# Queries and keys of the second attention: transposed in 32x32 blocks by VectorE and moved through DRAM, in place of TensorE transposes

## The chip, the cores and the metric

The kernel runs on one core of one Trainium2 chip. The core has TensorE (PE, matrix products, with its weight loads listed as PEld), VectorE (DVE), ScalarE (ACT), GpSimd (POOL) and SyncE (SP, which here only issues DMAs). Sixteen DMA engines move data between DRAM and the on-chip memory SBUF, and within SBUF. Matrix products are written to PSUM, which DMA does not touch here. The metric is the device time in microseconds (us) of one execution. All arithmetic is in 32-bit floats, in which a matrix product is issued as two passes.

## The reference

The input x has 8 sequences (b) of 128 tokens with 512 features. A first attention with small heads follows a per-sequence weight matrix, and its output is added to x. The second attention, on which the change bears, has 32 query heads and 8 key/value heads (groups) of 128 features, with a cache of 512 keys a sequence before the 128 own ones:

```python
q = jnp.einsum('bsd,ed->bse', x, Wq).reshape(bsz, seqlen, HQ, D)
k = jnp.einsum('bsd,ed->bse', x, Wk).reshape(bsz, seqlen, HK, D)
v = jnp.einsum('bsd,ed->bse', x, Wv).reshape(bsz, seqlen, HK, D)
q = _rmsnorm(q, q_norm_w)
k = _rmsnorm(k, k_norm_w)
q = _rope(q, pos)
k = _rope(k, pos)
kc = k_cache[block_table].reshape(bsz, L, HK, D)
vc = v_cache[block_table].reshape(bsz, L, HK, D)
k_all = jnp.concatenate([kc, k], axis=1)
v_all = jnp.concatenate([vc, v], axis=1)
scores = jnp.einsum('bqhd,bkhd->bhqk', q, k_all) * SCALE
scores = jnp.where(valid[:, None, None, :], scores, -1e+30)
probs = jax.nn.softmax(scores, axis=-1)
o = jnp.einsum('bhqk,bkhd->bqhd', probs, v_all)
return jnp.einsum('bse,de->bsd', o.reshape(bsz, seqlen, HQ * D), Wo)
```

Its output goes through a feed-forward layer (a dense matrix plus low-rank LoRA terms that depend on the sequence), whose result is added again.

## The kernel before

**Units.** The second attention is cut into 64 units (L141). A unit u is one group g of 4 query heads and one key/value head, for one sequence b. Units come in pairs: 2n and 2n+1 are two neighbouring groups of the same sequence, whose cached keys and values lie side by side and are gathered together by GpSimd (L149 to L166, four indirect DMAs for the keys and four for the values of a pair). The sequences run inside, the pairs of groups outside; so the weights of two groups are in use for 16 units, and the next two are loaded in time (L110 to L116).

**Order.** Every engine executes its instructions in the order in which the program writes them; there is no planner. The loop at L1052 is a software pipeline written by hand. In iteration u it writes the scores of unit u (L866), into which the projection of the queries of unit u+1 is woven (`between`, L1057, over `q_matmul`, L172), then the projection of keys and values of u+1 (L217), then the product of the probabilities of unit u-1 with the values (L956), and the output projection of u-1 (L976). In the last group the feed-forward of a finished sequence follows (L1007 to L1048) in every odd iteration from 51 on.

**A unit's steps.** The projected queries lie in PSUM as 128 tokens x 4 heads x 128 features. `q_turn` (L185) rotates them with tables of cosines and sines, already multiplied by the norm's weight, that stay in SBUF for all sequences (`ca`, `sa`, L110): three multiplications on VectorE, one addition on GpSimd, and the squares for the norm on ScalarE. `kv_turn` (L221) does the same for the keys. `norms` (L238) makes the factors from the squares, with a power on GpSimd between two steps of VectorE; the keys are scaled, the queries' factor is kept for the scores. The score product needs features on the partitions. So `queries` (L250) transposes the four heads on TensorE into PSUM (L254) and ScalarE copies them to SBUF (L256); `own_keys` (L268) does the same for the 128 own keys (L271, L273).

**Cached keys.** From unit 4 on they are transposed without TensorE: `turn_keys` (L834) has VectorE transpose them in 32x32 blocks, in odd iterations, behind `norms`; `move_keys` (L850) then moves the blocks to their partitions with 16 DMAs between SBUF tiles for a pair, 8 in each of two units, issued by SP after the third head's reduction (L923).

**Scores.** For each head r two products, with the queries as the stationary operand: 512 cached keys (L889) and 128 own keys (L896). VectorE adds the mask, scales and takes the row's minimum in one instruction (L902); ScalarE takes exponentials with their sum (L912) and divides (L880). PSUM has two buffers for scores, so the third head's product waits for the first head's reduction. VectorE then transposes the probabilities in blocks (L883), and 16 DMAs (L936) move the blocks to their partitions; the products with the values (L963), one iteration later, need all of them. In the last unit TensorE transposes the probabilities instead (L941).

**Behind the values.** VectorE copies the result out of PSUM (L971), TensorE multiplies it with the output weights (L982), and the sum over groups is kept in SBUF: copied by ScalarE for group 0 (L987), added by VectorE for the others (L989).

**Buffers.** The large intermediate tiles share a ring of 12 buffers (`tile_a`, L90). The first attention uses the same ring for the gathered weight matrices (`gather_w`, L292) and for the LoRA weights (`merge_loads`, L420).

## Time and profile before

| | us |
|---|---|
| median of 3 runs (1421.93 to 1422.63) | 1422.53 |
| the profiled execution | 1423.96 |
| its span, first to last instruction | 1421.1 |
| first score product of unit 0 | 220.6 |
| period of a unit in the middle | 17.8 |
| PE busy | 1391.5 |
| DVE busy | 931.8 |
| ACT busy | 655.9 |
| POOL busy | 568.2 |

The mean granted clock of TensorE is 0.997 of full speed. In a line of a group, the numbers after the bar are the busy time in us, the mean duration of one instruction in ns, and, after the next bar, the idle time of the engine just before them with what ended most of it. In a line of the timeline the columns are start in us, duration in us, engine, line, operation, the tiles (written <- read), the shape, and how many instructions were merged; in square brackets the engine's idle time before it and what ended it. A matmul's end is modelled and overlaps with the next one, so the distance from start to start says what it costs. "128*128" is the part of the array in use.

### The profile page before, as it was taken

The page shows a single profiled execution, that of the slowest core. Times are in us where ns is not written, and L with a number is a line of the kernel's source. Part 1 is how long each engine was busy: PE and PEld are TensorE (multiplying, and loading weights), DVE is VectorE, ACT ScalarE, POOL GpSimd, SP SyncE. Part 2 cuts the span into 40 slices and gives each one's busy share as a digit, 9 for nine tenths or more (in the row PEclk, how much of TensorE's full clock was granted, in tenths as well). Part 3 has the DMA queues.
Part 4 walks back from the last instruction along what each step waited for, and adds up shares of the span by engine and source line. Part 5 has one row for each costly group of instructions (what it writes and reads, how often), then busy time and mean ns, then how long its engine had stood idle before and what let it go on. Part 6 is the DMA issues. An engine that isn't in the chain of part 4 may idle for free.

```text
span 1421.1 us, 20290 instructions
## 1 busy us (share of the span) xinstructions
PE 1391.5 (98%) x6244; PEld 898.5 (63%) x6244; DVE 931.8 (66%) x2266; ACT 655.9 (46%) x1520; POOL 568.2 (40%) x553
## 2 busy tenths in 40 slices
PE   6999989999999999999999999999999999999998
PEld 6877755566666666666666666666666665666555
DVE  5777846566666666666666666666666665666651
ACT  3555535444444444444444444444444444344431
POOL 5774342433333333333333333333333433343220
PEclk9999999999999999999999999999999999999999
DMA  6255013444444565444445654444456544444440
GB/s 198 75 164 183 31 37 104 129 117 118 119 115 119 161 193 151 119 119 119 119 119 159 196 148 119 118 119 119 121 160 192 152 117 136 131 111 112 115 111 30
DMA packets 156202, 180.26 MB, mean 127 GB/s; under 512 B 92416, under 2 KB 97792, under 8 KB 156096
## 3 DMA queue, kind: packets, MB, share of 16 engines
q1 hardware_dynamic: 140544, 134.39, 34.0%
q0 software_dynamic: 15552, 44.58, 10.8%
q8 instruction: 50, 0.82, 0.2%
q14 instruction: 56, 0.46, 0.1%
HBM read 75.83 MB, written 4.72 MB: 57 GB/s over the span
## 4 chain that ended last, share of the span: by engine, by line
PE 93%; DVE 2%; issue 2%; DMA 1%; ACT 1%; POOL 1%; SPq 1%; another core or an unknown queue 0%; DVEq 0%; POOLq 0%; ACTq 0%
PE op L963 19%; PE qp L177 15%; PE sc L889 15%; PE yp L982 15%; PE kvp L217 7%; PE sc L896 4%; PE fp L1044 2%; PE hp L514 2%; PE qTp L254 2%; PE pT1p L638 2%; PE qp L530 2%; PE att L673 2%; PE o L657 1%; PE sc L595 1%; PE kvp L545 1%
## 5 line engine op out<-in xcount | busy, mean ns | idle before, releaser
L902 DVE CUSTOM_DVE_ANT_0 pr<-sc,mask,nq 128x640 f32<-128x640 f32 x256 | 226.0, 884 | 144.2 <-PE sc L896 90.9
L912 ACT ACTIVATE pr<-pr,nm 128x640 f32<-128x640 f32 x256 | 211.8, 827 | 189.3 <-DVE nm L902 102.1
L889 PE MATMUL sc<-kT,qT 128*128 128x512 f32 x512 | 262.0, 593 | 0.0
L177 PE MATMUL qp<-wq,x1T 128*128 128x512 f32 x512 | 251.2, 593 | 0.0
L963 PE MATMUL op<-pT,vg 128*128 128x256 f32 x1024 | 242.0, 379 | 1.6 <-DMA pT<-fl 1.6
L203 POOL TENSOR_TENSOR qa<-qa,qb 128x512 f32<-128x512 f32 x64 | 81.8, 1278 | 375.2 <-DVE sums L879 375.2
L982 PE MATMUL yp<-wo,oT 128*128 128x512 f32 x504 | 229.2, 598 | 2.0 <-DVE oT L971 2.0
L963 PEld LDWEIGHTS op<-pT,vg 128*128 128x128 f32 x1024 | 193.9, 190 | 27.8 <-DVE sums L879 1.8
L880 ACT ACTIVATE pr<-pr,sums 128x640 f32<-128x640 f32 x256 | 208.4, 814 | 0.0
L883 DVE STREAM_TRANSPOSE fl<-pr 128x640 f32<-128x640 f32 x252 | 189.2, 808 | 0.0
L896 PEld LDWEIGHTS sc<-kTo,qT 128*128 128x128 f32 x512 | 96.4, 190 | 124.4 <-issue 119.2
L982 PEld LDWEIGHTS yp<-wo,oT 128*128 128x128 f32 x504 | 91.4, 191 | 95.1 <-issue 91.5
L160 POOL DMA_INDIRECT kg<-in_k_cache_dram,idx_kv x128 | 131.6, 1029 | 35.3 <-issue 34.8
L160 POOL DMA_INDIRECT vg<-in_v_cache_dram,idx_kv x128 | 128.6, 1005 | 37.8 <-issue 33.6
L889 PEld LDWEIGHTS sc<-kT,qT 128*128 128x128 f32 x512 | 87.7, 191 | 80.2 <-issue 77.8
L256 ACT COPY qT<-qTp 128x512 f32<-128x512 f32 x64 | 37.5, 586 | 205.3 <-PE qTp L254 204.7
L217 PEld LDWEIGHTS kvp<-wkv,x1T 128*128 128x128 f32 x512 | 97.3, 190 | 40.5 <-issue 30.1
L217 PE MATMUL kvp<-wkv,x1T 128*128 128x256 f32 x512 | 121.0, 379 | 0.0
L244 POOL TENSOR_TENSOR rs<-ss,minus_half 128x5 f32<-128x5 f32 x64 | 76.5, 1196 | 83.1 <-DVE ss L242 82.2
L177 PEld LDWEIGHTS qp<-wq,x1T 128*128 128x128 f32 x512 | 82.8, 191 | 31.5 <-issue 31.5
L896 PE MATMUL sc<-kTo,qT 128*128 128x128 f32 x512 | 99.2, 275 | 0.0
L273 ACT COPY kTo<-kTp 128x128 f32<-128x128 f32 x64 | 17.1, 267 | 166.4 <-issue 115.2
(155 smaller groups left out, 1701.1 us busy)
## 6 DMA issues: line engine op xcount, KB each, us to landing
pT<-fl SPq DMA_DIRECT2D x1008, 80.0 KB
kT<-flk SPq DMA_DIRECT2D x480, 32.0 KB
wq<-in_wq_dram SPq DMA_DIRECT2D x8, 1024.0 KB
wo<-in_wo_dram SPq DMA_DIRECT2D x8, 1024.0 KB
wkv<-in_wkv_dram SPq DMA_DIRECT2D x8, 512.0 KB
kg<-in_k_cache_dram,idx_kv POOLq DMA_INDIRECT x128
vg<-in_v_cache_dram,idx_kv POOLq DMA_INDIRECT x128
res<-x_kept SPq DMA_DIRECT2D x8, 256.0 KB
```

Source lines behind the costliest of these rows:

```text
L160: nc.gpsimd.indirect_dma_start(out=dst[:, c].rearrange("p n d -> p (n d)"), out_offset=None, in_=src, in_offset=bass.IndirectOffsetOnAxis( ...
L177: nc.tensor.matmul(s["qp"][:].rearrange("p h d -> p (h d)"), x1T[b][:, c, :], weights[g][0][:, c, :], start=(c == 0), stop=(c == KC - 1),)
L203: nc.gpsimd.tensor_tensor(qa[:], qa[:], qb[:], ALU.add)
L217: nc.tensor.matmul(s["kp"][:], x1T[b][:, c, :], weights[g][1][:, c, :], start=(c == 0), stop=(c == KC - 1))
L880: nc.scalar.activation(prs[r][:], prs[r][:], AF.Copy, scale=sums[:, r : r + 1])
L883: nc.vector.transpose(s["flips"][:, :, :, r, :].rearrange("p b c j -> p c b j"), prs[r][:])
L889: nc.tensor.matmul(sc[:, : NBLK * P].rearrange("p (k j) -> p k j", j=32), s["qT"][:, r, :], s["kT"], start=True, stop=True,)
L896: nc.tensor.matmul(sc[:, NBLK * P : NK], s["qT"][:, r, :], s["kTo"][:], start=True, stop=True)
L902: nc.vector.tensor_tensor_reduce(out=pr[:], in0=sc[:, :NK], in1=mask[:], scale=s["nq"][:, r : r + 1], scalar=3.0e38, op0=ALU.add, op1=ALU.min,
L912: nc.scalar.activation(pr[:], pr[:], AF.Exp, bias=nm[:, r : r + 1], scale=-1.0, accum_out=sums[:, r : r + 1],)
L963: nc.tensor.matmul(ops[h][:, : 2 * S], cached(u, "vg", c) if c < NBLK else s["vo"][:], s["pT"][:, :, c, 2 * h : 2 * h + 2, :].rearrange("p ...
L982: nc.tensor.matmul(yp[:], s["oT"][:, r, :], weights[g][2][:, r, :], start=(r == 0), stop=(r == REP - 1))
```

## The change

From unit 4 on the queries and the own keys go the way of the cached keys. `turn_ahead` has VectorE transpose a unit's queries (128x512) and own keys (128x128) in 32x32 blocks: the queries into a tile that interleaves the two units of a pair element by element, the keys as a fifth block beside the four cached ones. `keys_out` writes the tile of the keys of a pair to DRAM with one DMA, and the queries with four, one for each group of 32 tokens, in pieces of 64 elements. `keys_in` reads both back, a partition block at a time, with 8 DMAs. The stationary operand of a score product is now every second element of the interleaved tile. These DMAs take the place of the 16 moves of cached keys of a pair.

Because the way is longer, a unit is projected 4 units ahead rather than 1: iterations 0 and 1 project units 1 to 5, every later one unit u+4, and iterations 60 to 63 none. More buffers are held for that (values 7, keys 3, factors 6), and room is made: the ring of large tiles has 9 buffers rather than 12, a few of its users get tiles of their own, and the tables of cosines and sines are kept in DRAM, from which each pair's part (128 x 2 KB) is loaded.

```diff
     def tile_a(shape, name):
-        return both.tile(shape, F32, tag="a", name=name, bufs=12)
+        return both.tile(shape, F32, tag="a", name=name, bufs=9)
...
-    ca = [one([P, B, D2], F32, f"ca_{n}") for n in range(2)]
-    sa = [one([P, B, D2], F32, f"sa_{n}") for n in range(2)]
+    tab_kept = dram.tile([B, P, 4, D2], F32, tag="tab", name="tab_kept")
+    tabs = {}
...
+    def load_tab(n):
+        if n < N // 2:
+            tabs[n] = both.tile([P, 4, D2], F32, tag="tab", name=f"tab_{n}")
+            nc.sync.dma_start(out=tabs[n][:], in_=tab_kept[n % B])
...
-        vo = both.tile([P, D2], F32, tag="vo", name=f"vo_{u}", bufs=3)
+        vo = both.tile([P, D2], F32, tag="vo", name=f"vo_{u}", bufs=7)
...
-        ka = both.tile([P, D2], F32, tag="ka", name=f"ka_{u}")
+        ka = both.tile([P, D2], F32, tag="ka", name=f"ka_{u}", bufs=3)
...
-                merge[key] = tile_a([RANK, DM], key)
+                merge[key] = p1.tile([RANK, DM], F32, tag=key, name=key, bufs=1)
...
     def turn_keys(n):
-        flk = p2.tile([P, 4, NBLK, 2, 32], F32, tag="flk", name=f"flk_{n}", bufs=1)
+        flk = p2.tile([P, 4, 2, NBLK + 1, 32], F32, tag="flk", name=f"flk_{n}", bufs=1)
...
+        flq = p2.tile([P, 4, REP, 32, 2], F32, tag="flq", name=f"flq_{n}", bufs=1)
+        kT = p2.tile([P, 4, 2, NBLK + 1, 32], F32, tag="kT2", name=f"kT2_{n}")
+        qT = p2.tile([P, REP, 4, 32, 2], F32, tag="qT2", name=f"qT2_{n}")
...
+            s["qT"] = [qT[:, r].rearrange("p a i m -> p (a i) m")[:, :, m] for r in range(REP)]
+            s["kTo"] = kT[:, :, m, NBLK]
+
+    def turn_ahead(v):
+        (flk, flq), m = pairs[v // 2]["fl"], v % 2
+        nc.vector.transpose(
+            flq[:, :, :, :, m].rearrange("p b r i -> p r b i"),
+            st[v]["qa"][:].rearrange("p r d -> p (r d)"),
+        )
+        nc.vector.transpose(flk[:, :, m, NBLK], st[v]["ka"][:])
+
+    def keys_out(n):
+        flk, flq = pairs[n]["fl"]
+        kk = dram.tile([P, 4, 320], F32, tag="kk", name=f"k_kept_{n}", bufs=2)
+        kq = dram.tile([32, 4 * REP, 4, 64], F32, tag="kq", name=f"q_kept_{n}", bufs=2)
+        nc.sync.dma_start(out=kk[:], in_=flk[:].rearrange("p b m c i -> p b (m c i)"))
+        for a in range(4):
+            nc.sync.dma_start(
+                out=kq[:, :, a],
+                in_=flq[32 * a : 32 * a + 32].rearrange("p b r i m -> p (b r) (i m)"),
+            )
+        pairs[n]["dr"] = [kk, kq]
+
+    def keys_in(n):
+        kT, qT = pairs[n]["to"]
+        kk, kq = pairs[n]["dr"]
         for b in range(4):
+            part = slice(32 * b, 32 * b + 32)
             nc.sync.dma_start(
-                out=pairs[n]["kT"][32 * b : 32 * b + 32, :, a].rearrange("p c m i -> p c (m i)"),
-                in_=pairs[n]["flk"][32 * a : 32 * a + 32, b].rearrange("p c m i -> p c (m i)"),
-            )
+                out=kT[part].rearrange("p a m c i -> p a (m c i)"),
+                in_=kk[:].rearrange("(a j) b x -> j b a x", j=32)[:, b],
+            )
+            nc.sync.dma_start(
+                out=qT[part].rearrange("p r a i m -> p (r a i m)"),
+                in_=kq[:, REP * b : REP * b + REP].rearrange("j r a x -> j (r a x)"),
+            )
     def pair_keys(u):
         if u == 2:
-            turn_keys(u)
+            turn_keys(2)
+            turn_ahead(4)
         if 1 < u < N - 2:
-            for a in range(u % 2 * 2, u % 2 * 2 + 2):
-                move_keys(u // 2 + 1, a)
+            if u % 2 == 0:
+                turn_ahead(u + 3)
+                keys_out(u // 2 + 1)
+            else:
+                keys_in(u // 2 + 1)
...
-        now, nxt, last = u < N, u + 1 < N, 1 <= u <= N
+        now, last = u < N, 1 <= u <= N
+        ahead = {0: [1, 2, 3], 1: [4, 5]}.get(u, [u + 4] if u + 4 < N else [])
...
-            norms(u + 1)
-            queries(u + 1)
-            for v in {0: (1,), 1: (2, 3)}.get(u, ()):
-                keys(v)
-            if u > 2 and u % 2 and u // 2 + 2 < N // 2:
-                turn_keys(u // 2 + 2)
+        if ahead:
+            norms(ahead[0])
...
+        if u > 2 and u % 2 and u // 2 + 2 < N // 2:
+            turn_keys(u // 2 + 2)
+            turn_ahead(u + 3)
...
         if u == 0:
+            project(2)
             flip_last(x1_last)
-        if nxt:
-            own_keys(u + 1)
-        if u == 0:
+            own_keys(1)
+            norms(2)
+            project(3)
+            queries(2)
+            own_keys(2)
+            norms(3)
+            load_tab(2)
+            load_tab(3)
             load_wo(1)
+        elif u == 1:
+            queries(3)
+            own_keys(3)
+            project(5)
+            norms(5)
+        if u % 2:
+            load_tab((u + 7) // 2)
```

`project(v)` writes the projections of unit v and their rotation one after the other, outside the scores. `pair_keys` is called after the third head's reduction.

## The prediction

> **What bounds the kernel now.** The page is read first: busy time of each engine, then the chain that ended last.
>
> ```profile
> PE 1391.5 (98%) x6244; PEld 898.5 (63%) x6244; DVE 931.8 (66%) x2266; ACT 655.9 (46%) x1520; POOL 568.2 (40%) x553
> ...
> PE 93%; DVE 2%; issue 2%; DMA 1%; ACT 1%; POOL 1%; SPq 1%; another core or an unknown queue 0%; DVEq 0%; POOLq 0%; ACTq 0%
> ```
>
> TensorE is busy for 98% of the span and owns 93% of the chain: a matmul less is time less, as long as its data are there. The groups of instructions on PE by line come next (count, then busy us and mean ns of one, then idle time before).
>
> ```profile
> L963 PE MATMUL op<-pT,vg 128*128 128x256 f32 x1024 | 242.0, 379 | 1.6 <-DMA pT<-fl 1.6
> ...
> L254 PE MATMUL qTp<-ident,qa 128*128 128x128 f32 x256 | 38.5, 273 | 1.8 <-POOL qa L203 1.8
> ...
> L271 PE MATMUL kTp<-ident,ka 128*128 128x128 f32 x64 | 17.5, 273 | 1.1 <-DVE ka L247 1.1
> ```
>
> L254 and L271 are the transposes that the change takes away. Their 273 ns overlap with their neighbours, so the price is read from starts in the timeline of PE, in a unit of the middle:
>
> ```profile
> 719.03 0.59 PE L963 MATMUL op<-pT,vo 128*128 128x256 f32 x2
> 719.46 0.60 PE L254 MATMUL qTp<-ident,qa 128*128 128x128 f32 x4
> 719.90 3.60 PE L982 MATMUL yp<-wo,oT 128*128 128x512 f32 x8
> 723.34 0.27 PE L271 MATMUL kTp<-ident,ka 128*128 128x128 f32 x1
> 723.45 1.02 PE L889 MATMUL sc<-kT,qT 128*128 128x512 f32 x2
> ...
> 726.47 1.02 PE L889 MATMUL sc<-kT,qT 128*128 128x512 f32 x2
> ...
> 732.93 1.89 PE L963 MATMUL op<-pT,vg 128*128 128x256 f32 x8
> ...
> 741.23 1.02 PE L889 MATMUL sc<-kT,qT 128*128 128x512 f32 x2
> ```
>
> From first score to first score a unit takes 741.23 - 723.45 = 17.8 us, without a hole. Four query transposes move the next start by 0.44 us (719.46 to 719.90), the key transpose by 0.11 (723.34 to 723.45). VectorE around the same boundary, and SP's queue:
>
> ```profile
> 722.01 1.42 DVE L840 STREAM_TRANSPOSE flk<-kg 128x256 f32<-128x256 f32 x4
> 723.54 0.69 DVE L989 TENSOR_TENSOR y<-yp,y 128x512 f32<-128x512 f32 x1
> 724.14 0.55 DVE L874 TENSOR_SCALAR mask<-place,lens_f 128x640 f32<-128x640 f32 x1
> 724.83 0.88 DVE L902 CUSTOM_DVE_ANT_0 pr<-sc,mask,nq 128x640 f32<-128x640 f32 x1
> ...
> 729.69 0.88 DVE L902 CUSTOM_DVE_ANT_0 pr<-sc,mask,nq 128x640 f32<-128x640 f32 x1 [0.97 <-PE sc L896]
> ...
> 732.75 3.00 DVE L883 STREAM_TRANSPOSE fl<-pr 128x640 f32<-128x640 f32 x4
> ```
>
> ```profile
> 718.03 10.89 SPq L936 DMA_DIRECT2D pT<-fl  x16
> 729.03 5.15 SPq L853 DMA_DIRECT2D kT<-flk  x8
> ```
>
> VectorE is gapless from its cache-key transposes to the score reduction (L902), but waits 0.97 us for PE inside the scores. SP spends 10 to 11 us of each unit on issuing the 16 moves of the probabilities and 5 on 8 moves of keys: 0.65 us each. The moves end at 728.92; their reader starts at 732.93. In the last unit that reader does wait, and the same two views price the way from issue to use:
>
> ```profile
> 1374.22 10.25 SPq L936 DMA_DIRECT2D pT<-fl  x16
> ```
>
> ```profile
> 1386.44 1.97 PE L963 MATMUL op<-pT,vg 128*128 128x256 f32 x8 [1.57 <-DMA pT<-fl]
> ```
>
> 1386.44 - 1384.47 = 2.0 us from last issue to use. So the probabilities are there 2.0 us early at 732.93 (2.8 one unit before).
>
> **The change part by part.** The sum is made against the profiled execution, 1423.96 us (span 1421.1), which lies 1.4 above the median of the runs.
>
> 1. *Transposes removed.* Units 4 to 63 lose 5 each: 60 x (0.44 + 0.11) = -33.0 us, all on the chain. [...] ACT loses two copies (L256 and L273, 0.59 + 0.27 us a unit); it is no bound.
>
> 2. *VectorE's block transposes added.* Four 128x640 in 3.00 us are 0.73 apart, four 128x256 in 1.42 are 0.34: about 1.03 ns an element, so 128x512 (queries) is 0.60 and 128x128 (keys) 0.20 us. The queries are written with a step of two elements, which no row shows: 0.60 by the nearest rows (contiguous writes), 1.2 if the step doubles it. I take 0.60. In even units the 0.80 us lie before the fourth reduction, under its 0.97 of waiting: nothing, and 0.75 more is idle before L200. In odd units they follow the cache-key transposes, in front of y, mask and the next unit's first reduction, which frees the score buffer of its third score matmul. From the rows: 722.01 + 1.42 + 0.80 = 724.23; y 0.60, mask 0.69, reduction 0.88 put its end at 726.40, some 0.1 later at PE. PE, 0.55 earlier than in its row, wants the buffer at 726.47 - 0.55 = 725.92: a stall of 0.6 us. It needs the y addition on VectorE (in units of group 0 ScalarE copies y, so not below unit 17) and no feed-forward behind (not from 51): 17 boundaries, +10.2 us; bounds 0 and 17 x 1.2 = 20.
>
> 3. *Strided stationary operand.* qT is read with a step of two elements by L889 and L896. A weight load has 0.43 us to hide under a 512-column pass, and 0.11 under the 128-column ones; 5 loads of qT a unit lie there. No row has such a step: 0 if it costs nothing, 60 x 5 x 0.11 = +33 if it doubles. I take 0, the value of all loads of the trace, which are contiguous.
>
> 4. *DMA.* A pair of units had 32 moves of probabilities and 16 of keys on SP; it gets 32, 5 writes to DRAM, 8 reads back and 1 table: 46 x 0.65 = 29.9 us of 34.5, less than the 31.2 before. In the changed kernel's order each DMA of this queue waits for the landing of the eighth before it, so the eighth move of the probabilities waits for the last query write. Times from an even unit's first score: transposes done at 6.1, writes issued by 9.3, moves from 12.4, the eighth at 17.0. The key write is 128 rows of 5 KB (about 2.3 us at the 144 ns that packets of 2560 bytes take in the packet records, 16 engines). The queries are 2048 pieces of 256 bytes, 128 an engine: 2.2 us at the 17 ns of 256-byte packets between SBUF tiles, the nearest in size; 10.8 us at the 84 ns of a 2048-byte write to DRAM, the nearest in target. They are usable at 6.1 + 2.0 + 2.3 + 2.2 = 12.6 by the first, before 17.0: hidden. I take the first, since a 2048-byte packet took 84 ns to SBUF and to DRAM alike. Reads are issued behind the moves and needed a unit later: hidden by that unit. Tables (2 KB x 128 a pair) are read two units ahead. Without cover the 14 issues would be 9 us a pair, the 1.2 MB read back another 4 at the 284 GB/s that the 2560-byte packets make. [...]
>
> 5. *Weight loads.* Around them the DMA engines are already 69 to 71% busy (windows 1043 to 1079 us, 198 to 206 GB/s, against 44% and 118 elsewhere), and 2.1 MB more a pair adds 60 GB/s. The 2.0 us of slack, 0.55 less after step 1, may go there: 12 loads of queries, keys and output weights; 0 to 15 us, I take half a us each, +6.
>
> 6. *Three projections moved from the end to the front.* A projection is 3.44 + 1.72 = 5.16 us of PE wherever it stands. At the front, before had about 6 us of holes in units 0 to 2 (one at L982, 2.0, "DVE oT"); the new order fills some and adds three waits of VectorE for the norms and a longer transpose in unit 2: -1 (bounds -5, +5). At the end units 60 to 62 lose the work that covered the softmax. From unit 60's first score: the last unit's rows give 4.6 us for bare scores, 7.3 to the last reciprocal, then 3.0 of transposes, 10.1 of issues, 2.0 to use: 22.4. Unit 60 is held by the copies behind the transposes (10.8, then 3.44 of L982): 14.3. In 61 the values wait until 22.4 instead of 19.4, and the feed-forward ends at 34.9; 62 ends like 60 at 49.1; the values of 62 start at 34.9 + 22.4 = 57.3, and 34.7 us follow as now (1386.44 to 1421.1): 92.0. Today it is 100.1 (from 1338.81 - 17.79); less the 15.5 of projections and 1.65 of transposes it would be 83.0. So +9.0.
>
> 7. *First block.* The ring of the shared tiles shrinks from 12 to 9, so three loads of LoRA weights wait on SP for the last conditioning matmul, as today the next two do (155.4 us); the gates behind them come some 3 us later, mostly while VectorE is held anyway: +1 (0 to 4).
>
> Sum: -33.0 + 10.2 + 0 + 0 + 6 - 1 + 9.0 + 1 = -7.8: 1416 us for the profiled execution, and against the median of the runs 1422.5 - 7.8 = 1414.7, so 1415 us.
>
> **The rivals.** *The stalls do not come* (steps 2, 5 and 7 at nothing, y or mask starting earlier than the rows say): -33 - 1 + 9 = -25, 1398 us. For it: only 0.6 us a boundary is missing. Against: the gapless rows of VectorE.
>
> *The DRAM writes hold the probabilities back* (slower). Place: the eighth move in even units. With a 256-byte write of t ns the last lands at 10.4 + 0.128 t; it decides when that passes 17.0 by more than the 2.0 us of slack, at t = 67 ns. At 84 ns the wait is 10.4 + 10.8 - 17.0 - 2.0 = 2.2 us a pair, 30 pairs, +65: 1480 us. Against it: 17 ns in the only 256-byte rows.
>
> *The strided load costs double* (slower): +33, 1448 us. For it: five exposed places; against: nothing slower in the trace.
>
> *DMA full or VectorE late beyond the bounds taken* (steps 2 and 5 at their ends): +19, 1434 us.
>
> **How the numbers follow.** Forecast 45%, stalls absent 20%, DRAM writes 13%, strided load 10%, crowding 12%. A measurement tells about 0.2% here, 2.8 us. The forecast's own range, 1405 to 1425, gives two thirds of its chance to faster, a fifth to the same. Faster: 0.30 + 0.20 = 0.50; the same 0.10; slower 0.40. The range 1395 to 1455 leaves out the far part of the DRAM case and little at the low end.
>
> **What would show it.** The unit's period should be 17.2 us, 17.8 in even units from 18 on, with waits of L889 for DVE there. Transposes on PE: 4 units' worth. VectorE's queries: 0.6 us each. In units 61 and 63 the values wait some 3 us for the moves. I am wrong if values wait for the moves throughout, if the score matmuls start farther apart than 1.08 us, or if weight loads of the scores take longer than 190 ns.

## The result and the profile after

The changed kernel takes 1440.25 us (median of 5 runs, 1434.99 to 1444.09) against 1421.93 us of the kernel before (1420.4 to 1422.63): 1.0123 times as long, with a 95% interval of 1.0096 to 1.015. The prediction said 1415 us, some 0.5% faster; the kernel is 1.2% slower. The profiled execution is the fastest of the five, 1434.99 us, with a span of 1433.2 us against 1421.1 us before.

The page of the changed kernel, the lines that answer to those shown of before (busy time of the engines, the chain that ended last, the queue of SP):

```profile
PE 1375.8 (96%) x5944; PEld 876.6 (61%) x5944; DVE 974.1 (68%) x2386; ACT 599.9 (42%) x1400; POOL 555.3 (39%) x553
...
q1 hardware_dynamic: 167792, 199.93, 52.1%
...
HBM read 119.61 MB, written 42.21 MB: 113 GB/s over the span
...
PE 79%; DMA 6%; DVE 5%; SPq 4%; issue 2%; ACT 1%; POOL 1%; another core or an unknown queue 0%; DVEq 0%; POOLq 0%; ACTq 0%
```

On the page of the kernel before, the queue of SP (packets, MB, share of the 16 engines' time) and the traffic with DRAM (HBM in the profile) are:

```profile
q1 hardware_dynamic: 140544, 134.39, 34.0%
...
HBM read 75.83 MB, written 4.72 MB: 57 GB/s over the span
```

TensorE has lost 300 matmuls, as promised, but only 16 us of busy time, and it owns 79% of the chain instead of 93%: DMA, VectorE and SP's issues hold 15% now. The waits of TensorE name them (us in total, times, longest):

```profile
PE sc L944 <- DMA pT<-fl: 9.0, 5, 3.3
PE op L1022 <- DMA pT<-fl: 8.8, 4, 2.8
...
PE sc L944 <- DVE nm L961: 5.7, 3, 5.0
...
PE yp L1041 <- DVE oT L1030: 3.4, 2, 1.8
...
PE sc L944 <- DMA qT<-q_kept: 1.5, 1, 1.5
```

The kernel before had one wait of its values for the moves (1.6 us) and none of its scores for a DMA. The two spans, cut at the first scores of units 0, 4 and 60 (from the timelines of TensorE; the last columns are two of the runs below):

| stretch, us | before | after | after without the later weight loads | last version |
|---|---|---|---|---|
| start to unit 0 | 220.6 | 224.6 | 226.0 | 219.6 |
| units 0 to 3 | 75.0 | 95.0 | 92.7 | 90.2 |
| units 4 to 59 | 1025.4 | 1018.7 | 1001.2 | 1000.2 |
| unit 60 to the end | 100.1 | 94.9 | 96.3 | 91.9 |
| span | 1421.1 | 1433.2 | 1416.2 | 1401.9 |

Some 15.5 us of projections (three of the prediction's 5.16 us) moved from the last stretch to the second. The 56 units of the middle were to become 14.6 us shorter and became 6.7 shorter. Up to unit 50 the period from first score to first score is 17.79 us before (17.93 in every second unit up to 17), with one exception of 19.76 (unit 49 to 50). After, it is 17.26 to 17.35 us, and from unit 20 on 17.64 (18.00 once) behind odd boundaries, that is, into odd units; but the stretches that end at units 12, 14, 18, 28, 29, 34, 44 and 50 take 18.3 to 22.7. All of these lie within three units behind a load of weights. The one that ends at unit 12 (18.94 us), in SP's queue and at TensorE (start, duration, instruction, idle time before it and what ended it):

```profile
446.65 0.52 SPq L136 DMA_DIRECT2D wq<-in_wq_dram  x1
447.27 0.51 SPq L137 DMA_DIRECT2D wkv<-in_wkv_dram  x1
447.83 0.49 SPq L901 DMA_DIRECT2D kT<-k_kept  x1
...
450.62 0.43 SPq L905 DMA_DIRECT2D qT<-q_kept  x1
452.17 0.31 SPq L901 DMA_DIRECT2D kT<-k_kept  x1
454.15 0.31 SPq L905 DMA_DIRECT2D qT<-q_kept  x1
455.05 7.16 SPq L995 DMA_DIRECT2D pT<-fl  x11
```

```profile
454.68 3.62 PE L1041 MATMUL yp<-wo,oT 128*128 128x512 f32 x8
459.79 1.10 PE L944 MATMUL sc<-kT,qT 128*128 128x512 f32 x2 [1.50 <-DMA qT<-q_kept]
```

1.5 MB of weights stand in front of the eight reads of the next pair's keys and queries. In the packet records the engines move weights until 453 and the last piece of the reads lands at 458.9; TensorE stands still for 1.5 us and starts at 459.79. Away from the loads, up to unit 48, the reads land 3.5 to 4.4 us ahead of the first score. So the reads do not have a unit of time in hand, as the prediction took them to have, but about 4 us. The profile names the moves (`pT<-fl`) for most waits of scores, but a score product reads only keys and queries; by the packets the last read of the pair lands 1.1 to 1.3 us before the late first scores of units 18, 28, 34, 44 and 50, as it does 0.9 us before that of unit 12.

The longest stretch, to unit 18 (22.72 us), has two loads of 1 MB of output weights, one ahead of the writes of queries and the moves, one behind them:

```profile
537.18 0.05 SPq L143 DMA_DIRECT2D wo<-in_wo_dram  x1
...
537.84 7.38 SPq L890 DMA_DIRECT2D q_kept<-flq  x4
545.32 12.35 SPq L995 DMA_DIRECT2D pT<-fl  x16
557.77 0.53 SPq L143 DMA_DIRECT2D wo<-in_wo_dram  x1
```

```profile
559.84 2.96 PE L1022 MATMUL op<-pT,vg 128*128 128x256 f32 x8 [2.31 <-DMA pT<-fl]
...
570.57 1.10 PE L944 MATMUL sc<-kT,qT 128*128 128x512 f32 x2 [1.06 <-DMA pT<-fl]
```

Behind the first load the writes take 7.38 us to issue instead of 3.7, the moves start late, and the product with the values waits 2.31 us; behind the second the reads are late, and the score waits 1.06 us.

### The profile page after: what moved, and what is told of

It reads as the page before. It is cut to its first block, busy times and chain, and to the rows that moved or that the text cites. A ratio compares the mean times of both kernels' runs of the same rounds, so it can differ in the third digit from the quotient of the medians.

```text
span 1433.2 us, 19490 instructions
## 1 busy us (share of the span) xinstructions
PE 1375.8 (96%) x5944; PEld 876.6 (61%) x5944; DVE 974.1 (68%) x2386; ACT 599.9 (42%) x1400; POOL 555.3 (39%) x553
## 4 chain that ended last, share of the span: by engine, by line
PE 79%; DMA 6%; DVE 5%; SPq 4%; issue 2%; ACT 1%; POOL 1%; another core or an unknown queue 0%; DVEq 0%; POOLq 0%; ACTq 0%
PE op L1022 16%; PE qp L183 13%; PE sc L944 13%; PE yp L1041 11%; PE kvp L223 6%; PE sc L951 3%; SPq L995 3%; PE hp L526 2%; PE fp L1103 2%; PE pT1p L650 2%; DMA kT<-k_kept 2%; DMA pT<-fl 2%; PE att L685 2%; PE qp L542 1%; DMA qT<-q_kept 1%
## 5 line engine op out<-in xcount | busy, mean ns | idle before, releaser
L944 PE MATMUL sc<-kT,qT 128*128 128x512 f32 x512 | 267.4, 604 | 17.9 <-DMA pT<-fl 9.0
L1022 PE MATMUL op<-pT,vg 128*128 128x256 f32 x1024 | 245.2, 383 | 8.8 <-DMA pT<-fl 8.8
L951 PEld LDWEIGHTS sc<-kT,qT 128*128 128x128 f32 x480 | 94.6, 197 | 112.4 <-issue 112.4
L944 PEld LDWEIGHTS sc<-kT,qT 128*128 128x128 f32 x512 | 93.5, 197 | 112.8 <-issue 91.6
L166 POOL DMA_INDIRECT vg<-in_v_cache_dram,idx_kv x128 | 124.4, 972 | 40.2 <-issue 31.9
L166 POOL DMA_INDIRECT kg<-in_k_cache_dram,idx_kv x128 | 123.9, 968 | 35.3 <-issue 34.2
L951 PE MATMUL sc<-kT,qT 128*128 128x128 f32 x480 | 94.2, 278 | 0.0
L641 POOL TENSOR_TENSOR pr<-pr,sums 128x1024 f32<-128x1024 f32 x32 | 60.0, 1897 | 76.4 <-DVE sums L640 58.6
L630 ACT ACTIVATE pr<-sc,nm 128x128 f32<-128x128 f32 x256 | 67.7, 415 | 33.1 <-DVE nm L616 33.1
```

The costliest lines, as they stand in the source:

```text
L166: nc.gpsimd.indirect_dma_start(out=dst[:, c].rearrange("p n d -> p (n d)"), out_offset=None, in_=src, in_offset=bass.IndirectOffsetOnAxis( ...
L944: nc.tensor.matmul(sc[:, : NBLK * P].rearrange("p (c a j) -> p c a j", c=NBLK, j=32), s["qT"][r], s["kT"], start=True, stop=True,)
L951: nc.tensor.matmul(sc[:, NBLK * P : NK].rearrange("p (a j) -> p a j", j=32), s["qT"][r], s["kTo"], start=True, stop=True,)
L1022: nc.tensor.matmul(ops[h][:, : 2 * S], cached(u, "vg", c) if c < NBLK else s["vo"][:], s["pT"][:, :, c, 2 * h : 2 * h + 2, :].rearrange("p ...
```

## The experiments

All ratios are to the kernel before, run in turn on the same chip; intervals are 95%. From one set of runs to another its median lay between 1414.5 and 1421.9 us, so ratios are compared, not times.

| run | median, us | ratio |
|---|---|---|
| changed kernel | 1440.25 | 1.0123 [1.0096, 1.0150] |
| before, no transposes | 1394.16 | 0.9811 [0.9796, 0.9826] |
| changed, no later weights | 1416.06 | 0.9960 [0.9944, 0.9975] |
| before, no later weights | 1418.52 | 0.9979 [0.9970, 0.9987] |
| gather later | 1433.22 | 1.0080 [1.0061, 1.0098] |
| weights, ScalarE's queue | 1479.37 | 1.0454 [1.0441, 1.0467] |
| queries adjacent | 1428.46 | 1.0108 [1.0090, 1.0126] |
| turned inside the scores | 1426.11 | 1.0080 [1.0067, 1.0093] |
| tail on two queues | 1431.59 | 1.0123 [1.0109, 1.0138] |
| weights, GpSimd's queue | 1460.63 | 1.0272 [1.0248, 1.0296] |
| together, weights by GpSimd | 1444.14 | 1.0183 [1.0150, 1.0216] |
| together, weights as they were | 1425.69 | 1.0031 [1.0019, 1.0043] |
| weights ahead of the moves | 1425.41 | 1.0091 [1.0063, 1.0118] |
| together, weights ahead | 1413.45 | 0.9997 [0.9982, 1.0011] |
| together, weights in even units | 1403.65 | 0.9920 [0.9906, 0.9933] |

The theory was that the weight loads, behind the longer traffic on SP's queue, cost most of what is missing, and the gathers of GpSimd in the front and the moves in the tail the rest. The rivals were the traffic through DRAM itself, the strided weight load, and VectorE.

**The transposes alone.** In the kernel before, from unit 4 on, TensorE's transposes and ScalarE's copies behind them are left out:

```diff
     def queries(u):
         s = st[u]
+        if u > 3:
+            s["qT"] = s["qa"]
+            return
...
     def own_keys(u):
         s = st[u]
+        if u > 3:
+            s["kTo"] = s["ka"]
+            return
```

> The kernel before with the query and key transposes of units 4 to 63 left out altogether (TensorE's five, and ScalarE's two copies; scores are computed from untransposed queries and keys, which is wrong). It prices the first step of the prediction alone. By the pitch of their starts, 0.55 us a unit: -33 us, ratio 0.977. By the 273 ns of their records, 1.37 us a unit: -82 us, ratio 0.942. If the units are held by VectorE once TensorE is faster: less than 25 us, with waits of the scores for VectorE.

The ratio is 0.9811, -27 us. The period falls from 17.79 to 17.25 us, 0.54 us, as the pitch of the starts had it. Some of it is lost again in the units behind the last load of output weights, whose three periods are 17.97, 19.48 and 18.86, 4.6 us over the others together, where the kernel before lost 2.0: a faster TensorE alone makes that load felt more. So the first step of the prediction is shown, within 6 us.

**The weight loads.** In the changed kernel and in the one before, the loads for groups 2 to 7 are left out:

```diff
     def load_qkv(g):
+        if g > 1:
+            weights[g] = weights[g - 2][:2]
+            return
...
     def load_wo(g):
+        if g > 1:
+            weights[g].append(weights[g - 2][2])
+            return
```

> The changed kernel without the loads of query, key/value and output weights for the key groups 2 to 7 (groups 0 and 1 are used again, so the second attention is computed with the wrong weights for those groups). Theory (weight loads): in the changed kernel the periods of units 12 to 14, 18, 28, 29, 34, 44 and 50 are together about 18 us over those of their neighbours, all within three units behind such a load, since moves behind 1 MB on the same queue land late and there is little slack left: the time should fall by 15 to 20 us against the changed kernel (ratio to before 0.998 to 1.002), and all periods from unit 4 to 50 should be 17.3 or 17.6. Rival (the added traffic through DRAM itself, at any time): less than 6 us, long units stay, elsewhere perhaps.

> The control: the kernel before without the same loads (groups 0 and 1 used again). Its periods are 17.79 throughout, but for one unit of 19.76 behind the load of output weights: theory -2 us (ratio 0.9985). A fall of 10 us or more would mean that the loads cost both kernels alike, through TensorE reading SBUF while it is written, and not through the queue.

The loads cost the changed kernel 1.6% (1.0123 to 0.9960, some 23 us) and the kernel before 0.2% (3 us). Without them all periods from unit 4 to 50 are 17.25 to 17.35 or 17.63 to 17.69, with one of 18.00, and the middle is 24.2 us shorter than before. So the 37 MB more that go to DRAM and back hold nothing by themselves; it is the loads that no longer fit. The rival falls.

The waits of TensorE between units 4 and 60 of the changed kernel say where: 10.5 us at the first scores of units 12, 18, 28, 34, 44 and 50, which need the reads, 3.3 us at two products with the values (before 487.92 and 559.84), which need the moves. Two holes among these are followed by half clock (last section), an estimated 1.7 us each. Together that is 17.2 of the 17.5 us by which these 56 units take longer than without the loads.

**The front.** Four of the eight gathers go behind the projection of unit 5:

```diff
-        if u % 2:
+        if u % 2 and u > 1:
             gather(u // 2 + 1, "vg")
...
             norms(5)
+            gather(1, "vg")
```

> The changed kernel, with the second gather of iteration 1 (values of the cache for pair 1) issued by GpSimd behind the projection of unit 5 instead of ahead of it. Theory (front): in the changed kernel the third score of unit 2 waits 5.0 us for VectorE, whose norms of unit 5 wait for GpSimd, which had eight gathers of 1.2 us ahead of the rotation's additions; TensorE then runs 6.8 us at half clock. With four gathers less ahead, the wait should fall below 1 us and the half clock with it: 7 to 8 us less than the changed kernel (ratio to before 1.012 -> about 1.007). Rival (VectorE itself is late in unit 2 through the two added transposes and four cache transposes, GpSimd only looks like the cause): no more than 1 us less, the wait of 5 us stays.

In the changed kernel, GpSimd, VectorE and TensorE around the third score of unit 2:

```profile
277.76 0.94 POOL L166 DMA_INDIRECT vg<-in_v_cache_dram,idx_kv  x1 [0.30 <-issue]
278.72 1.28 POOL L209 TENSOR_TENSOR qa<-qa,qb 128x512 f32<-128x512 f32 x1
```

```profile
283.04 0.17 DVE L251 TENSOR_SCALAR nq<-rs 128x4 f32<-128x4 f32 x1 [1.65 <-POOL rs L249]
...
284.01 0.88 DVE L961 CUSTOM_DVE_ANT_0 pr<-sc,mask,nq 128x640 f32<-128x640 f32 x1
```

```profile
284.95 2.07 PE L944 MATMUL sc<-kT,qT 128*128 128x512 f32 x2 [5.02 <-DVE nm L961]
```

The addition of unit 5's queries starts the moment the eighth gather ends, and the chain through norms and mask to the reduction ends in TensorE's wait. With four gathers moved, the wait of 5.02 us is 2.21 us, the period 21.48 instead of 25.57 us, and the ratio 1.0080. The median fell by 0.43%, 6 us, the period by 4.1 us. But the wait of 5.02 us is the longest of its kind: in the seven other profiles with the gathers in their old place it is 3.6 us (six of them) or 4.3 us, and 2.2 us in all five with four gathers moved. So the chain is shown, and these four gathers are worth 1.4 us or more of the wait; what makes up the rest of the 6 us is not, and the wait did not fall below 1 us, as the theory had it.

**The stride of the queries.** TensorE loads 128 adjacent elements in place of every second one:

```diff
-            s["qT"] = [qT[:, r].rearrange("p a i m -> p (a i) m")[:, :, m] for r in range(REP)]
+            s["qT"] = [
+                qT[:, r].rearrange("p a i m -> p (a i m)")[:, m * P : m * P + P] for r in range(REP)
+            ]
```

> The changed kernel, with TensorE loading 128 adjacent elements as queries instead of every second one (the scores then belong to mixed tokens of two units, which is wrong; all else is the same). It prices the third step of the prediction alone. By that step's choice 0. By the starts of the scores, 1.09 to 1.10 us apart instead of 1.08, some 2 to 4 us less. By a doubled load: 33 us less. The periods tell it best: 17.29 and 17.35 us stay or become 17.25 and 17.32 (as in the kernel before without transposes).

The ratio, 1.0108, can't be told from 1.0123, but the periods are clean: 17.25, 17.32 and 17.62 against 17.29, 17.35 and 17.64, 0.03 us a unit, 2 us in all. The weight loads of the scores take 191 to 192 ns instead of 197. So the stride costs 2 us; the rival of a doubled load is refuted.

**VectorE at odd boundaries.** The transposes of an odd boundary go into the next unit's scores:

```diff
+            if r == 1 and u > 3 and u % 2 == 0 and u + 2 < N:
+                turn_ahead(u + 2)
...
             turn_keys(u // 2 + 2)
-            turn_ahead(u + 3)
```

> The changed kernel, with the block transposes of queries and own keys that VectorE did behind the cache-key transposes at the end of an odd iteration moved into the next unit's scores, ahead of its third reduction, where VectorE waits for TensorE. It prices the second step of the prediction. Theory (VectorE late at odd boundaries): the periods of even units from 20 on fall from 17.64 to 17.29, 16 of them, 5 to 6 us less. By the prediction's own 0.6 us a boundary: 10 us. Rival (the 0.35 us come from the y addition or the matmul for scores waiting for its reads): nothing, or a loss where the third reduction is now late.

All periods of 17.64 became 17.29 and the ratio 1.0080, 6 us less. The stall was VectorE's, at the 17 boundaries that the prediction named, but worth 0.35 us each and not 0.6. In the changed kernel the reduction that frees the buffer ends 3.21 us after the first score, where the prediction had reckoned 3.50:

```profile
889.62 0.67 DVE L878 STREAM_TRANSPOSE flq<-qa 128x512 f32<-128x512 f32 x1
890.21 0.26 DVE L882 STREAM_TRANSPOSE flk<-ka 128x128 f32<-128x128 f32 x1
890.40 0.65 DVE L1048 TENSOR_TENSOR y<-yp,y 128x512 f32<-128x512 f32 x1
890.98 0.53 DVE L929 TENSOR_SCALAR mask<-place,lens_f 128x640 f32<-128x640 f32 x1
891.65 0.88 DVE L961 CUSTOM_DVE_ANT_0 pr<-sc,mask,nq 128x640 f32<-128x640 f32 x1
```

(The first score of that unit starts at 889.32, the transpose with the step of two is 0.59 us from its successor: the step costs VectorE nothing.)

**The tail.** Half of the moves of units 60 to 62 are issued by ScalarE:

```diff
+                queue = nc.scalar if u >= N - 4 and k % 2 else nc.sync
-                nc.sync.dma_start(
+                queue.dma_start(
```

> The changed kernel, with half of the 16 moves of the probabilities of units 60 to 62 issued by ScalarE instead of SP. Theory (tail): with no projection left to cover them, the values of units 60 and 62 wait 2.7 and 2.8 us for the last move, whose issues take 10.1 us one behind the other; with two queues they are all issued some 5 us earlier, both waits go, and the half clock behind the second with them: 5 to 7 us less; from the first score of unit 60 to the end 94.9 becomes 88 to 90 us. Rival (the moves are held by their transfer, not by the issue): the waits stay, within 2 us of the changed kernel.

Nothing: 1.0123, and 95.0 us from unit 60 to the end instead of 94.9. The wait of unit 62 is gone, but that of unit 60 is 3.45 instead of 2.66 us, and ScalarE, which now issues moves, comes late to a copy:

```profile
1353.43 2.93 PE L1023 MATMUL op<-pT,vg 128*128 128x256 f32 x8 [3.45 <-DMA pT<-fl]
...
1362.41 0.43 PE L1089 MATMUL axp<-yT,a_eff 128*32 128x128 f32 x8 [2.73 <-ACT yT L1072]
```

For units 60 and 61 issuing on ScalarE only turns one wait into another; for unit 62 it pays. Later runs keep it for unit 62 alone.

**Another queue for the weights.** First ScalarE's, then GpSimd's:

```diff
-        nc.sync.dma_start(out=wq[:], in_=wq2[:, e].rearrange("(c p) e -> p c e", p=P))
+        queue = nc.scalar if g > 1 else nc.sync
+        queue.dma_start(out=wq[:], in_=wq2[:, e].rearrange("(c p) e -> p c e", p=P))
```

(wkv and wo alike; nc.gpsimd in the second run.)

> The changed kernel, with the twelve loads of weights for key groups 2 to 7 issued from ScalarE's queue instead of SP's, at the same places. Leaving the loads out brought the changed kernel from 1440 to 1416 us, and the kernel before from 1421 to 1418.5. Theory (queue order): the probabilities, and the writes and reads of queries and keys, land late because they stand behind 1 to 1.5 MB in the same queue, which every eighth landing holds up; with the loads in a queue of their own most of it comes back: 1417 to 1424 us, periods of 17.3 or 17.6 around the loads. Rival (bandwidth): the 16 DMA engines are shared by all queues, the load takes its share wherever it is issued: 1434 to 1440 us, long units of 18 to 22 us stay.

> The changed kernel, with the twelve loads of weights for key groups 2 to 7 issued from GpSimd's queue. From ScalarE's queue they made it 3% slower than the changed kernel: there the sixth move of a unit's probabilities was issued at 459.98, just behind the last packet of a weight load of the other queue (459.6), since the two queues share the eight semaphores whose landing every eighth issue waits for, and ScalarE issued the load late, behind its own work. GpSimd's issues have semaphores of their own. Theory (order and the shared eight landings): with neither in common the keys, queries and probabilities no longer stand behind the weights: ratio to before 0.997 to 1.003, long units of 18 to 22 us gone. Rival (bandwidth of the 16 engines, which all queues share): ratio 1.008 to 1.015, the long units stay.

Both theories of the first run missed: 1.0454, far over what either said. With the loads on ScalarE's queue the values waited 53.5 us for their moves. The issues of one unit's 16 moves, and ScalarE meanwhile:

```profile
448.75 18.08 SPq L997 DMA_DIRECT2D pT<-fl  x16
```

```profile
453.83 0.59 ACT L1048 COPY y<-yp 128x512 f32<-128x512 f32 x1 [7.85 <-PE yp L1043]
453.83 0.37 ACTq L137 DMA_DIRECT2D wq<-in_wq_dram  x1
```

The moves take 18 us instead of 10: the fifth is issued at 451.32, the sixth at 459.98, 0.4 us behind the last packet of the load that ScalarE issued at 453.83. In this run's trace both queues count their landings on the same eight semaphores (100 to 107), which the 1547 DMAs of SP in the changed kernel take in turn, 193 or 194 on each, and the moves wait each for the DMA before them on their semaphore. The sixth move's is 106, and the DMA before it on 106 is that load of ScalarE's: SP was held by a load of the other queue. From GpSimd's queue, whose semaphores (111 to 118) are its own, the ratio is still 1.0272, above both expectations again. There the load starts while a unit's moves are under way:

```profile
445.11 0.85 POOL L137 DMA_DIRECT2D wq<-in_wq_dram  x1
445.93 0.84 POOL L138 DMA_DIRECT2D wkv<-in_wkv_dram  x1
```

```profile
436.66 10.70 SPq L997 DMA_DIRECT2D pT<-fl  x16
```

```profile
456.16 3.75 PE L1024 MATMUL op<-pT,vg 128*128 128x256 f32 x8 [4.87 <-DMA qT<-q_kept]
```

The last of these moves is issued at 447.4 and lands, by the packet records, at 454.4, 7.0 us later instead of 1.2 (the median of the changed kernel); the values wait 4.87 us (the profile names the reads that were issued next; the packets say that the moves themselves were late). On SP's queue the load would have stood behind the moves.

**Small steps together.** The gather, the transposes and unit 62, with the weights by GpSimd and as they were:

> The changed kernel with the weights from GpSimd's queue, the gather behind the projection of unit 5, the odd transposes inside the next unit's scores, and half of unit 62's moves of probabilities from ScalarE's queue (in an earlier run that took away the wait of unit 62, while for units 60 and 61 it brought a new one). If the weights come free of the queue order, the gains add up: -0.4% (gather), -0.4% (transposes), -1.2% (weights), -0.3% (unit 62) against the changed kernel's 1.0123: ratio 0.987 to 0.992. If bandwidth holds: about 1.000 to 1.003.

> The same without the move of the weight loads to GpSimd's queue (they stay on SP's). The gather, the transposes and unit 62 together should give -1.0% to -1.2% against the changed kernel: ratio 1.000 to 1.003, with the long units behind the loads left. The difference to the run with all four is what the weight loads cost by their place in SP's queue.

1.0183, above both of its expectations, and 1.0031: the three small edits are worth 0.9%, and GpSimd's queue costs 1.5% here as it did alone. The long periods stay (in the second run 19.01 at unit 12, 22.88 at 18).

**The place in the queue.** The loads of SP's queue go ahead of a unit's moves, where SP is idle for 2 us, not behind them:

```diff
+    def moves(u):
+        s = st[u]
         for a in range(4):
             for k in range(4):
...
             after[1]()
+        for n in range(2):
+            g = (u + 4 - n) // (2 * B) * 2 + 2 + n
+            if (u + 4 - n) % (2 * B) == 2 * B - 2 and g < NKV:
+                load_qkv(g)
+            g = (u - 2 - n) // (2 * B) * 2 + 2 + n
+            if u > n + 1 and (u - 2 - n) % (2 * B) == 2 * B - 2 and g < NKV:
+                load_wo(g)
+        if u < N - 1:
+            moves(u)
```

The loads at the end of the iteration go.

> The changed kernel, with the twelve weight loads still on SP's queue, but issued ahead of a unit's moves of probabilities instead of behind them (wo one unit later, ahead of the moves of unit 16, 17 and so on). SP is idle there for about 2 us, the keys and queries of the next pair have been read or written before, and the 16 moves need only 4.6 us of the engines for 10.1 us of issues, so they can catch up. Both other queues made it worse (1.045 and 1.027): a load that starts while moves are under way takes the engines from them. Theory (what stands behind the load counts, not the bandwidth as such): the reads of keys and queries no longer land 5 us late, units 12, 14, 18, 28, 34, 44 and 50 lose most of their 18 us; a stall of about 1 us may stay where the load holds the moves: ratio 0.998 to 1.004. Rival (the engines have no room for 1 to 1.5 MB in a unit, wherever it stands): ratio 1.009 to 1.015, the long units move but stay.

> The same with the gather behind the projection of unit 5, the odd transposes inside the next unit's scores, and half of unit 62's moves from ScalarE's queue, which together gave 1.0031 with the loads in their old place. If the place of the loads is worth 12 to 17 us, this is 0.991 to 0.995 and beats the kernel before; if the engines have no room, 1.000 to 1.004.

1.0091, inside the rival's range, and, with the small edits, 0.9997, at its lower end: as the rival said, the long units moved but stayed. But the periods tell even units from odd ones. In the first run those that end at units 12, 18, 28, 34 and 50 and had been long are 17.28 or 17.29 us now; those at 13, 29, 45 and 51 are 18.80, 19.36, 21.99 and 21.74. Loads ahead of an even unit's moves cost nothing there (in the second run 0.6 us at 12 and 0.7 at 28); in an odd unit, where the keys and queries have just been read, they hold the moves. So the loads of odd groups went to even units, their output weights in two halves:

```diff
-            g = (u + 4 - n) // (2 * B) * 2 + 2 + n
-            if (u + 4 - n) % (2 * B) == 2 * B - 2 and g < NKV:
+            g = (u + 4 - 2 * n) // (2 * B) * 2 + 2 + n
+            if (u + 4 - 2 * n) % (2 * B) == 2 * B - 2 and g < NKV:
                 load_qkv(g)
...
+        if new:
+            load_wo(g, slice(0, REP // (1 + u % 2)))
         if u < N - 1:
             moves(u)
+        if new and u % 2:
+            load_wo(g, slice(2, REP))
```

> As the last run (all four edits, loads ahead of the moves), but the loads of an odd key group's query and key weights go ahead of the moves of the next even unit (12, 28, 44) instead of an odd one (11, 27, 43), and its output weights in two halves, ahead of and behind the moves of unit 17, 33, 49. In the run before, loads ahead of an even unit's moves cost nothing (periods of 12, 18, 28, 34, 50: 17.28), while those of an odd unit, where 1.15 MB of keys and queries are read just before, made the unit two later 1.5 to 4.7 us longer, some 13 us together. Theory (only what stands behind a load counts; in odd units reads, load and moves together do not fit): at least 6 to 10 us less, ratio 0.992 to 0.996. Rival (bandwidth: the cost moves to the even units): ratio 0.998 to 1.002.

0.9920 [0.9906, 0.9933]: 1403.65 us beside 1414.56 us of the kernel before. This version beats both. Load, moves and reads of one pair, in SP's queue:

```profile
423.94 0.58 SPq L136 DMA_DIRECT2D wq<-in_wq_dram  x1
424.65 0.44 SPq L137 DMA_DIRECT2D wkv<-in_wkv_dram  x1
426.03 11.55 SPq L1002 DMA_DIRECT2D pT<-fl  x16
437.63 0.58 SPq L903 DMA_DIRECT2D kT<-k_kept  x1
...
441.08 0.43 SPq L907 DMA_DIRECT2D qT<-q_kept  x1
443.42 10.04 SPq L1002 DMA_DIRECT2D pT<-fl  x16
```

The 16 moves are issued in 11.55 us behind the same 1.5 MB, 1.5 us more than without, and the reads behind them are not held (0.42 to 0.58 us each). The engines carry the same bytes in the same number of units; so most of the cost was not their bandwidth but what stood behind the load. Not all of it is gone: the periods ending at 18, 28 and 44 are still 19.28, 18.67 and 18.52. The 56 units of the middle took 1001.2 us without the later loads, which would be 994.9 without VectorE's 6.3 us of stalls; here they take 1000.2. So some 5 us of the loads' cost remain, which no run took further; whether bandwidth holds these is open.

## Why the prediction was wrong

1. *Transposes removed*, -33.0: right. The period fell by 0.54 us where nothing else was changed; the whole run gave -27 (30.4 us between the profiled executions, where 2.6 went at the weight loads); what took the rest of the medians' 6 us is not shown. The 273 ns of their records would have made it -82: in a stream of transposes the pitch of the starts, 0.55 us for five, decided rightly.
2. *VectorE at odd boundaries*, +10.2: right in mechanism and in the count of 17 boundaries, too large in size: 0.35 us each, 6 us.
3. *Strided stationary operand*, 0: it costs 2 us. Both signs that the prediction named showed, scores 1.09 us apart and weight loads of 197 ns, but they are worth 0.03 us a unit.
4. *DMA*: the writes to DRAM are hidden. The packets of 256 bytes took 20 ns in the mean, 18% over the 17 ns taken (18 ns in the median of either kernel), far from the 84 of the other bound, and no period in even units grew with them. What failed is the sentence on the reads: "Reads are issued behind the moves and needed a unit later: hidden by that unit." They have 3.5 to 4.4 us; a load of 1.5 MB takes 5 (from 448 to 453 in the packet records).
5. *Weight loads*, +6 with bounds 0 and 15: here the prediction fell. By the ratios they cost 23 us in the changed kernel against 3 before, 20 more; in the middle of the profiled executions 17.5 against 2, 15.5 more: at the upper bound or over it. The step counted what was left of the slack of the probabilities, by the bandwidth; it did not ask, load by load, what the queue holds behind it. There the reads stand, and behind them the writes of queries (four issues of 7.38 us instead of 3.7 behind the load at 537.18), and behind those the moves.
6. *Front and tail*: the tail was +9.0, ending 92.0 us from unit 60; it is 94.9, with the two waits where the prediction had them (2.66 and 2.82 us). The front was to take about 14 us more and takes 20. The prediction listed "three waits of VectorE for the norms" but priced nothing behind GpSimd, whose queue the projection of unit 5 was moved past: eight gathers, a wait of 5.0 us (3.6 in most other runs).
7. *First block*, +1: the profile has +4.0, but the start of unit 0 lies between 218.2 and 226.9 us in runs that share this block, so a microsecond can't be told here.

The middle closes. Without the later loads it is 24.2 us shorter than before: 56 x 0.54 = 30.2 saved; 6.3 of stalls (15 of 0.35, one of 0.40, one of 0.72); 2 of stride; and the 2 us of before's own long unit: -30.2 + 6.3 + 2 - 2 = -23.9. With the loads it is 6.7 shorter, 17.5 less. The prediction's sum with the sizes of the profiled execution in place of its own is -33.0 + 6.3 (stalls, not 10.2) + 2 (stride, not 0) + 15.5 (loads, 17.5 less the 2 of before, not 6) + 5 (front, not -1) + 12 (tail, not 9) + 4 (first block, not 1) = +12, against a measured 1433.2 - 1421.1 = +12. Of the miss of 20 us the loads are about half, the front almost a third. The medians lie 18 us apart, since the profiled execution is the fastest of its five; what makes up the other 6 is not shown. Of the rivals the one called crowding came nearest (1434 us, steps 2 and 5 at their ends), but partly by luck: step 2 was smaller than it took, step 5 at its end or over, and the front and the tail, which it left alone, were larger.

## What to carry to other kernels

When a change lengthens what a DMA queue carries, go through every large transfer on it and ask for each which deadline of those behind it comes first and how many microseconds it has in hand; the slack of one stream (here the probabilities) says nothing of another (the reads, about 4 us against 5 us of load). Moving a large load to another queue took away the order that protected the urgent transfers (1.0454 and 1.0272 instead of 1.0123); moving it within the queue, to where the transfers behind it have room, left some 5 us of its cost and turned 1.0031 into 0.9920. And a step that is moved on one engine is moved past what stands in the queues of all the others that it uses, the issues of GpSimd among them (eight gathers of 0.94 to 1.03 us here).

## What the runs showed of the hardware

A hole of TensorE of 2.0 us cost more than itself. In these stretches of the changed kernel (length, busy time of each engine, granted clock, DMA share, GB/s) the clock is 0.51 right behind the holes of 5.0 us (before 284.95) and of 2.3 us (before 559.84):

```profile
284.00:291.00 7.00, 6.04 (x10) 2.95 (x11) 5.37 (x15) 4.09 (x8) 0.00 (x0) 0.51 0.00 0
291.00:298.00 7.00, 7.00 (x31) 5.42 (x30) 6.25 (x17) 3.37 (x8) 1.38 (x2) 1.00 0.64 169
...
560.60:564.10 3.50, 3.50 (x10) 2.79 (x9) 3.31 (x8) 0.00 (x0) 0.46 (x1) 0.51 1.01 306
```

In the clock records the half clock lasts 6.83 us behind the first and 3.41 us behind the second, and by the granted share it takes up to an estimated half of that, 3.4 or 1.7 us, of matmuls with it. Holes of 2.0 (before 747.47) and 2.8 us (before 1396.46) were followed by it too, for 3.41 us each, one of 3.3 us (before 1139.1) and one of 2.7 (before 1361.01) were not, nor was any of the shorter holes behind the start of unit 0 (1.0 to 1.8 us). So the length of the hole alone does not tell here whether the clock falls, which goes with the spread of the changed kernel, 9 us over five runs at mean clocks of 0.988 to 0.992, where the kernel before, run beside it, keeps within 2.2 us (up to 5.4 over 17 executions elsewhere) and the last version, at 0.998 in its profile, within 2.6 us; that the clock is the whole of the spread is not shown.
